# Strided PSUM writes for layer 0's aggregate and layer 1's turned sums in a two-layer graph attention kernel

## The chip, the cores and the metric

The kernel runs on one core of a Trainium2 chip. The metric is the device time of one execution in microseconds (us). The kernel before was timed three times: 2320.42, 2313.36 and 2315.58 us, median 2315.58. A core has five engines with a queue each: TensorE (PE; its weight loads are listed apart as PEld), VectorE (DVE), ScalarE (ACT), GpSimd (POOL) and SyncE (SP). Products of TensorE land in PSUM; VectorE and ScalarE move them from there to SBUF, which is called evicting them here.

## The reference

There are 16 graphs of 1024 nodes with 256 features, and an adjacency `adj` of zeros and ones per graph. Two layers follow each other, each with a residual and a layer norm around it:

```python
# layer 0, per graph
Wh  = h @ W.T
att = ei[:, None] + ej[None, :]          # ei = Wh @ a1, ej = Wh @ a2
att = bn(att); att = leaky(att); att = bn(att)
att = softmax(att, axis=2) * adj
h_prime = elu(bn(att @ Wh))              # batch norm over all graphs and nodes
x = layernorm(x + h_prime)

# layer 1, per graph and per head h of 4
fts    = x @ W[h]
coefs  = alpha * softmax(leaky(f1[:, None] + f2[None, :]) + mask(adj)) \
       + (1 - alpha) * softmax(adj)
out[h] = elu(coefs @ fts + x)
x = layernorm(x + mean_over_heads(out))
```

## The kernel before, in words

**Layer 0, the stage around the change (lines 523 to 656).** The scores are kept transposed, with keys on the 128 partitions. For graph b and key block k of 8, `weights(b, k)` makes a tile of 128 keys by 1024 queries: ScalarE scales (L534), VectorE takes the leaky maximum (L537), ScalarE exponentiates (L538), VectorE multiplies by the mask into `em` (L542, 11 buffers), and VectorE adds the unmasked weights into the running sum `sm` (L546, L548). `aggregate(b, hf, k)` multiplies: for each half `hf` of 512 queries and each half `oc` of the features, eight products over k accumulate into one PSUM bank `pa` (L578; four banks). A product in fp32 is recorded as two matmul instructions. `divisors(b)` sums `sm` over the partitions with 16 instructions (L555), takes the reciprocal on VectorE (L560), spreads it over all partitions by transposes of a broadcast column (L565), and ScalarE copies these from PSUM into `rd` (L570), two copies of 512 columns per graph. `store(b, hf)` evicts: VectorE multiplies each bank by `rd` with a sum as a by-product (L594), four times per graph, and ScalarE squares for the batch norm's variance (L603). The order of nodes in `hb` is permuted: query 8q + k is stored in column block k at place q. In the kernel before, L594 reads PSUM and `rd` in order and writes `hb` with a step of 128 elements.

The loop over b issues graph b's 16 groups of products with graph b+1's `weights` in between, `store(b - 1, 1)` after the second group, and `divisors(b + 1)` at the end. In this layer a planner, which works with estimated costs, arranges the instructions into each engine's queue before the launch; in layer 1 the order is written out by hand.

**Layer 1 (lines 1043 to 1849).** Only the neighbours are fetched: for each graph, lists of neighbours are built from the adjacency's bits (`Lists`), and rows of a table in DRAM are gathered by GpSimd's indirect DMA (L1341). A graph has 8 chunks `it`, each with 5 blocks of 25 nodes, and 4 heads in two pairs, so 16 units of (chunk, head pair), 256 units in all. Per unit: products of the weights with the fetched rows give sums `pu` (L1565); ScalarE divides them into `s` (L1631); `turn` multiplies each of the 5 blocks of `s` by the small matrix `MX`, which transposes the block and mixes the two softmaxes, into the one PSUM buffer `pt` (L1637, ten instructions of 100 columns); `turned` copies `pt` into `sT` on ScalarE (L1647); `linear` multiplies by the weights (L1659, eight instructions); VectorE adds x (L1667); ScalarE exponentiates (L1673); VectorE folds the heads (L1680 to L1688); the layer norm and the store follow. The loop at L1827 runs these as a pipeline: in step n, `turn` and `turned` work on unit n − 3, `linear` on unit n − 5, `add` and `exps` on unit n − 6.

In the kernel before, `pt` is laid out block by block (block, head, place), written in order by each product; `sT` needs node LO + 5q + n of a head at place (head, q, n), so the copy reads PSUM in order and writes SBUF with a step of five elements. Between the units stand the side works of the next graphs: scaling of eight node groups on ScalarE (L1485), the cast of list words (L1184), the residual's transposes (L1438) with their evictions (L1448, L1455), and the building of lists on VectorE. The last, rest block of each graph has its own turn (L1583), which the change leaves alone.

Of the kernel before, what the change touches and what calls it, by code (L numbers as in the profile page):

```python
# [8 lines left out]
F32 = mybir.dt.float32  # L9
# [10 lines left out]
P = 128  # L20
# [7 lines left out]
def kernel(  # L28
# [29 lines left out]
    nc = tc.nc  # L58
    B, N, F = x.shape
    H = W.shape[0]  # L60
    K = N // P
    C = F // P
    HALF = 512
    NH = N // HALF
# [46 lines left out]
    QB, NB = 25, 5  # L111
    NQ = K * NB + 1
    LEVELS = [1] * (NQ - 1) + [3]
    LO = 2
# [91 lines left out]
    with ExitStack() as l0:  # L206
# [10 lines left out]
        def small(pool, name, shape):  # L217
            return pool.tile([P, *shape], F32, name=name)
# [5 lines left out]
        with tc.tile_pool(name="apool", bufs=1) as apool, tc.tile_pool(  # L224
            name="aps", bufs=2, space=PSUM
# [14 lines left out]
            for name, v in (  # L240
# [3 lines left out]
                n = v.shape[0] // P  # L244
# [15 lines left out]
            for fc in range(C):  # L260
# [7 lines left out]
                for oc in range(C):  # L268
# [4 lines left out]
                        start=(oc == 0),  # L273
                        stop=(oc == C - 1),
# [4 lines left out]
            for b in range(B):  # L279
                wx = apool.tile([P, K, FX], F32, tag="wx", name=f"wx_{b}", bufs=3)  # L280
                for kk in range(K // KK):
# [10 lines left out]
                    for k in range(KK):  # L292
                        pw = aps_w.tile([P, FX], F32, tag="w", name=f"pw0_{b}_{kk}_{k}")
                        for fc in range(C):
                            nc.tensor.matmul(  # L295
                                pw, xT[:, k, fc, :], WX[:, fc, :],
                                start=(fc == 0), stop=(fc == C - 1),
# [26 lines left out]
        with tc.tile_pool(name="bpool", bufs=1) as bpool, tc.tile_pool(  # L324
            name="bps", bufs=2, space=PSUM
# [46 lines left out]
            q = small(qpool, "q", [K, B])  # L372
# [58 lines left out]
            for b in range(B):  # L431
# [17 lines left out]
                for k in range(K):  # L449
                    for it in range(K):  # L450
                        nc.tensor.matmul(
                            pt[:, k, 0:7], ds[it][:, k * P : (k + 1) * P], powers[:, b, it, 0:7],
                            start=(it == 0), stop=(it == K - 1),
# [69 lines left out]
        with tc.tile_pool(name="wk", bufs=1) as wk, tc.tile_pool(  # L523
            name="ps_a", bufs=4, space=PSUM
# [4 lines left out]
            ems, es, sm, rd, hb = ({} for _ in range(5))  # L529
# [21 lines left out]
            def divisors(b):  # L551

                pd = ps_s.tile([P, K], F32, tag="s", name=f"pd_{b}")
                for it in range(K):
                    nc.tensor.matmul(  # L555
                        pd[:, it : it + 1], sm[b][:, it * P : (it + 1) * P], ones[:, 0:1],
                        start=True, stop=True,
                    )
                r = wk.tile([P, K], F32, tag="rc", name=f"rc_{b}", bufs=2)
                nc.vector.reciprocal(r, pd)  # L560
                rd[b] = wk.tile([P, N], F32, tag="rd", name=f"rd_{b}", bufs=2)
                for hf in range(NH):
                    ps = ps_s.tile([P, HALF], F32, tag="s", name=f"prd_{b}_{hf}")
                    for k in range(KH):
                        nc.tensor.transpose(  # L565
                            ps[:, k * P : (k + 1) * P],
                            r[:, hf * KH + k : hf * KH + k + 1].to_broadcast([P, P]),
                            ident,
                        )
                    nc.scalar.copy(rd[b][:, hf * HALF : (hf + 1) * HALF], ps)  # L570

            acc = {}

            def aggregate(b, hf, k):
                for oc in range(C):
                    if k == 0:
                        acc[b, hf, oc] = ps_a.tile([P, HALF], F32, tag="a", name=f"pa_{b}_{hf}_{oc}")
                    nc.tensor.matmul(  # L578
                        acc[b, hf, oc],
                        wh[b][:, k, oc * P : (oc + 1) * P],  # L580
                        ems[b, k][:, hf * HALF : (hf + 1) * HALF],
                        start=(k == 0),
                        stop=(k == K - 1),
                    )

            def store(b, hf):
                if hf == 0:
                    hb[b] = wk.tile([P, C, N], F32, tag="hb", name=f"hb_{b}", bufs=2)
                half = slice(hf * HALF, (hf + 1) * HALF)
                part = hb[b].rearrange("p c (k q) -> p c k q", k=K)[:, :, :, hf * P // 2 : (hf + 1) * P // 2]  # L590
                n = b * NH + hf
                sums3 = wk.tile([P, C], F32, tag="sums3", name=f"sums3_{b}_{hf}", bufs=2)
                for oc in range(C):
                    nc.vector.tensor_tensor_reduce(  # L594
                        out=part[:, oc].rearrange("p k q -> p q k"),
                        in0=acc[b, hf, oc].rearrange("p (q k) -> p q k", k=K),
                        in1=rd[b][:, half].rearrange("p (q k) -> p q k", k=K), scale=1.0,
                        scalar=0.0, op0=ALU.mult, op1=ALU.add, accum_out=sums3[:, oc : oc + 1],
                    )
                nc.vector.tensor_scalar(mn3[:, n, :], sums3, -1.0 / HALF, None, ALU.mult)  # L600
                for oc in range(C):
                    dist = wk.tile([P, K, P // 2], BF16, tag="dist", name=f"dist_{b}_{hf}_{oc}", bufs=2)
                    nc.scalar.activation(  # L603
                        dist, part[:, oc], AF.Square, bias=mn3[:, n, oc : oc + 1], scale=1.0,
                        accum_out=sq3[:, n, oc : oc + 1],
                    )
                if hf == NH - 1:
                    nc.sync.dma_start(h_dram[b], hb[b])
# [7 lines left out]
            for b in range(B):  # L616
                for n in range(NH * K):
                    hf, k = divmod(n, K)
                    aggregate(b, hf, k)
                    if b == 0 and n == K + 2:  # L620
                        divisors(0)
                    if n == K + 4:
                        casts.behind(hb[b][0:1, 0, 0:1])
                    if n == 1 and b + 2 < B:
                        mts[b + 2] = mask(mpool, b + 2, "mt0")
                    if n == 1 and b > 0:
                        store(b - 1, NH - 1)
                    if n == (K + 1 if b else K + 3):
                        store(b, 0)
                    if n % 2 == 0 and b + 1 < B:  # L630
                        weights(b + 1, n // 2)
                    if n == 2 and b + 2 < B:
                        queries(b + 2)
                    if n == 3 and b == 4:
                        shifted1()
                if b + 1 < B:
                    divisors(b + 1)
                if b + 2 < B:
                    load(b + 2)
            store(B - 1, NH - 1)  # L640

            mv3 = wk.tile([P, C, 2], F32, name="mv3")
# [400 lines left out]
    with ExitStack() as l1:  # L1043
# [4 lines left out]
        ps_t = l1.enter_context(tc.tile_pool(name="ps_t", bufs=1, space=PSUM))  # L1048
# [12 lines left out]
        QR = (H + 1) * QB  # L1061
        MX = pk.tile([P, H, QB], F32, name="MX")
# [321 lines left out]
        class Graph:  # L1384
# [49 lines left out]
            def turn(self, k):  # L1434

                pz = self.pz[k] = ps_s.tile([P, C, TW], F32, tag="s", name=f"pz_{self.b}_{k}")
                for oc in range(C):
                    nc.tensor.matmul(  # L1438
                        pz[:, oc, :], self.h[:, oc, k * P : (k + 1) * P], IW[:, oc, :],
                        start=True, stop=True,  # L1440
                    )
# [153 lines left out]
        class Unit:  # L1595
# [36 lines left out]

            def turn(self):

                self.pt = ps_t.tile([P, NB, H, QB], F32, tag="t", name=f"pt_{self.nm}")
                for i in range(NB):
                    nc.tensor.matmul(  # L1637
                        self.pt[:, i].rearrange("p h q -> p (h q)"),
                        self.first.s[0:QR, i, self.hp * P : (self.hp + 1) * P],
                        MX[0:QR].rearrange("p h q -> p (h q)"), start=True, stop=True,  # L1640
                    )

            def turned(self):
                f, u = self.first, self.it
                if self.hp == 0:
                    f.sT = pk.tile([P, C, H, P], F32, tag="sT", name=f"sT_{self.nm}", bufs=2)
                nc.scalar.copy(  # L1647
                    f.sT[:, self.hp, :, LO : LO + NB * QB].rearrange("p h (q n) -> p n h q", n=NB), self.pt
                )
                if self.hp == 1:  # L1650
                    sl = self.g.sl[:, :, :, 3 * u : 3 * u + 3]
                    nc.scalar.copy(f.sT[:, :, :, 0:LO], sl[:, :, :, 0:LO])
                    nc.scalar.copy(f.sT[:, :, :, P - 1 : P], sl[:, :, :, LO:3])
# [96 lines left out]
        def side(g):  # L1750
# [11 lines left out]
            for hf in range(2):  # L1762
                after[AT["rw", hf]] += [each(lists.load_rows, hf)]
                turned(AT["words", hf], lists.words, lists.worded, hf)
            early[AT["used"]] += [lists.used]
            turned(AT["places"], lists.places, lists.placed)
            for part in range(4):
                early[AT["low"][part]] += [each(lists.low, part)]
# [128 lines left out]
```

## Time and profile before

| | |
|---|---|
| median of three runs | 2315.58 us |
| profiled execution, its own time | 2355.05 us |
| its span | 2353.3 us |
| mean granted TensorE clock | 0.924 |
| busy: TensorE, VectorE, ScalarE, GpSimd | 2032.3, 1851.5, 1537.4, 929.0 us |
| layer 0's products L578 | 323.8 to 832.8 us of the span |
| layer 1's turns L1637 | 949.4 to 2323 us of the span |
| L578, 512 columns | 1024 instructions |
| L594, 512 elements | 64 instructions, median 1049 ns |
| L570, 512 elements | 32 instructions, median 586 ns |
| L1637, 100 columns | 2560 instructions |
| L1647, 500 elements | 256 instructions, median 1059 ns |

[...]products overlap; how long one holds TensorE is read from the distance of the starts. The profiled execution is one single execution and was longer than the three timed ones.

### The profile page before, as it was taken

To read this page: it belongs to the slowest core of one execution; us is meant where nothing else is said; L and a number is where in the kernel's file an instruction comes from. 1 tells how busy PE (TensorE), PEld (TensorE's weight loads), DVE (VectorE), ACT (ScalarE), POOL (GpSimd) and SP (SyncE) were. 2 spreads that over 40 slices of the span, in tenths; PEclk is the share of its full clock that TensorE was granted. 3 is DMA by queue.
4 is the path that set the end of the run, shared out by engine and by line. 5 is a ranking of instruction groups with operands and counts; after the bars stand their busy time and mean duration, and the time that the engine had idled before them with its cause. 6 is when DMAs were issued, how large, how long until landed. Compare 5 with 4: busy or idle time off the path is not lost. (4 is left out here: it accounts for less than half of the span.)

```text
span 2353.3 us, 35722 instructions
## 1 busy us (share of the span) xinstructions
PE 2032.3 (86%) x12023; PEld 1572.7 (67%) x12023; DVE 1851.5 (79%) x4480; ACT 1537.4 (65%) x3156; POOL 929.0 (39%) x1005
## 2 busy tenths in 40 slices
PE   6685468999999943899999998999998999999995
PEld 5574334444444432787887887887887887887885
DVE  3234799999999754598889888798898888898885
ACT  1111667777777522668877877868877868868775
POOL 0000100000000004456667666666666657667671
PEclk9897569999999965899999999999999999999998
DMA  8697979996555134646756755756755756756550
GB/s 244 186 275 182 279 150 208 214 215 166 150 161 152 72 121 147 178 150 161 208 162 167 205 158 151 205 162 160 208 161 152 200 166 161 202 166 159 142 147 24
DMA packets 344669, 404.68 MB, mean 172 GB/s; under 512 B 189929, under 2 KB 291357, under 8 KB 334237
## 3 DMA queue, kind: packets, MB, share of 16 engines
q1 hardware_dynamic: 293533, 258.40, 38.1%
q0 software_dynamic: 49728, 141.39, 24.9%
q10 hardware_dynamic: 1216, 2.51, 0.3%
q8 instruction: 98, 1.61, 0.3%
q14 instruction: 94, 0.77, 0.1%
HBM read 330.90 MB, written 104.88 MB: 185 GB/s over the span
## 5 line engine op out<-in xcount | busy, mean ns | idle before, releaser
L1341 POOL DMA_INDIRECT xc<-xe_dram,ix x640 | 683.6, 1068 | 209.7 <-issue 173.7
L1659 PE MATMUL pv<-W1s,sT 128*128 128x256 f32 x2048 | 504.1, 390 | 1.8 <-issue 0.9
L578 PE MATMUL pa<-em,wh 128*128 128x512 f32 x1024 | 451.9, 599 | 18.1 <-issue 13.4
L1659 PEld LDWEIGHTS pv<-W1s,sT 128*128 128x128 f32 x2048 | 380.5, 196 | 45.6 <-issue 1.3
L1637 PEld LDWEIGHTS pt<-MX,s 125*128 125x128 f32 x2560 | 343.7, 202 | 44.7 <-ACT sT L1647 15.4
L578 PEld LDWEIGHTS pa<-em,wh 128*128 128x128 f32 x1024 | 194.2, 192 | 251.0 <-issue 240.1
L1637 PE MATMUL pt<-MX,s 125*128 125x100 f32 x2560 | 346.9, 285 | 15.3 <-ACT sT L1647 8.5
L1565 PE MATMUL pu<-xc,w 128*125 128x256 f32 x1280 | 348.7, 391 | 5.5 <-issue 4.5
L1647 ACT COPY sT<-pt 128x500 f32<-128x500 f32 x256 | 271.8, 1062 | 104.2 <-PE pt L1637 90.2
L1631 ACT ACTIVATE s<-pu,z 125x256 f32<-125x256 f32 x640 | 259.6, 472 | 44.3 <-DVE z L1623 27.8
L1673 ACT ACTIVATE m<-v,neg 128x512 f32<-128x512 f32 x256 | 183.7, 718 | 155.4 <-DVE v L1667 99.5
L1565 PEld LDWEIGHTS pu<-xc,w 128*125 128x125 f32 x1280 | 232.4, 191 | 42.7 <-issue 11.3
L534 ACT ACTIVATE e<-eb,c,s 128x1024 f32<-128x1024 f32 x128 | 155.0, 1236 | 80.2 <-DVE sm L548 41.9
L1716 POOL TENSOR_TENSOR ors<-ors,mhalf 128x1 f32<-128x1 f32 x128 | 105.7, 826 | 223.1 <-DVE ors L1710 216.4
L1667 DVE TENSOR_TENSOR v<-pv,x 128x512 f32<-128x512 f32 x256 | 175.0, 684 | 11.8 <-PE pv L1659 9.7
L538 ACT ACTIVATE e<-e,v,u 128x1024 f32<-128x1024 f32 x128 | 152.3, 1229 | 30.6 <-DVE e L537 24.5
L1438 PE MATMUL pz<-IW,h 128*128 128x136 f32 x512 | 89.7, 306 | 79.9 <-DVE fs L1455 37.7
L542 DVE TENSOR_TENSOR em<-e,mt 128x1024 f32<-128x1024 f32 x128 | 155.6, 1220 | 2.3 <-ACT e L538 1.3
L295 PE MATMUL pw<-WX,xT 128*128 128x266 f32 x512 | 130.5, 410 | 28.9 <-DVE wx L299 13.8
L537 DVE SCALAR_TENSOR_TENSOR e<-e 128x1024 f32<-128x1024 f32 x128 | 151.6, 1219 | 0.0
L299 DVE COPY wx<-pw 128x266 f32<-128x266 f32 x128 | 54.7, 434 | 117.3 <-PE pw L295 90.9
L291 ACT COPY xT<-px 128x512 f32<-128x512 f32 x64 | 34.5, 588 | 166.9 <-PE px L285 166.9
(301 smaller groups left out, 3180.5 us busy)
## 6 DMA issues: line engine op xcount, KB each, us to landing
x<-in_x_dram SPq DMA_DIRECT2D x32, 1024.0 KB
adj<-in_adj_dram POOLq DMA_DIRECT2D x16, 2048.0 KB
rw<-adj SPq DMA_DIRECT2D x32, 1024.0 KB
A<-u_dram SPq DMA_DIRECT2D x128, 250.0 KB
xe_dram<-x SPq DMA_DIRECT2D x16, 1060.0 KB
wh_dram<-wx SPq DMA_DIRECT2D x16, 1024.0 KB
wh<-wh_dram SPq DMA_DIRECT2D x16, 1024.0 KB
h_dram<-hb SPq DMA_DIRECT2D x16, 1024.0 KB
```

Source lines behind the costliest of these rows:

```text
L534: nc.scalar.activation(e, ebs[b], AF.Identity, bias=c1[:, k, b : b + 1], scale=s1[:, k : k + 1])
L538: nc.scalar.activation(e, e, AF.Exp, bias=v2[:, k : k + 1], scale=u2[:, k : k + 1])
L542: nc.vector.tensor_tensor(em, e, mts[b][:, k, :], ALU.mult)
L578: nc.tensor.matmul(acc[b, hf, oc], wh[b][:, k, oc * P : (oc + 1) * P], ems[b, k][:, hf * HALF : (hf + 1) * HALF], start=(k == 0), stop=(k ...
L1341: nc.gpsimd.indirect_dma_start(out=self.xc[:, i, :], out_offset=None, in_=xe_dram[g.b % 2], in_offset=bass.IndirectOffsetOnAxis(ap=g.l.ix[ ...
L1565: nc.tensor.matmul(pu[0:QR, 0:F], c.w[:, k].rearrange("p h q -> p (h q)"), c.xc[:, k, 0:F], start=(i == 0), stop=(i == len(OF[q]) - 1),)
L1631: nc.scalar.mul(f.s[0:QR, i], f.pu[i][0:QR, 0:F], f.z[0:QR, i : i + 1])
L1637: nc.tensor.matmul(self.pt[:, i].rearrange("p h q -> p (h q)"), self.first.s[0:QR, i, self.hp * P : (self.hp + 1) * P], MX[0:QR].rearrange ...
L1647: nc.scalar.copy(f.sT[:, self.hp, :, LO : LO + NB * QB].rearrange("p h (q n) -> p n h q", n=NB), self.pt)
L1659: nc.tensor.matmul(self.pv[:, hh, :], self.first.sT[:, fc, self.hp * HP + hh, :], W1s[:, fc, self.hp * HP + hh, :], start=(fc == 0), stop= ...
L1667: nc.vector.tensor_tensor(self.v2, self.pv, self.g.x[:, self.it].unsqueeze(1).to_broadcast([P, HP, F]), ALU.add)
L1673: nc.scalar.activation(self.m, self.v2, AF.Exp, bias=neg1, scale=1.0)
```

## The change

Both places get the same exchange of orders. The product writes its columns into PSUM with a step, at the place where the eviction will want them, and the eviction then reads and writes runs of neighbouring elements.

Layer 0: the bank `pa` is laid out as (k, q), 8 by 64. A product still reads its 512 query columns in order (q, then k), and writes them with a step of 64 elements. L594 then reads PSUM in order and writes runs of 64. Its second operand `rd` must have the same order, so L570 now reads PSUM with a step of eight elements and writes in order.

Layer 1: `pt` is laid out as (head, q, block). Each of the five block products writes its 100 columns with a step of five elements; L1647 reads PSUM in order and writes four runs of 125. The number of instructions, of bytes and of buffers stays as it was everywhere.

```diff
-                rd[b] = wk.tile([P, N], F32, tag="rd", name=f"rd_{b}", bufs=2)
+                rd[b] = wk.tile([P, NH, K, P // 2], F32, tag="rd", name=f"rd_{b}", bufs=2)
...
-                    nc.scalar.copy(rd[b][:, hf * HALF : (hf + 1) * HALF], ps)
+                    nc.scalar.copy(rd[b][:, hf], ps.rearrange("p (q k) -> p k q", k=K))
...
-                        acc[b, hf, oc] = ps_a.tile([P, HALF], F32, tag="a", name=f"pa_{b}_{hf}_{oc}")
+                        acc[b, hf, oc] = ps_a.tile([P, K, P // 2], F32, tag="a", name=f"pa_{b}_{hf}_{oc}")
                     nc.tensor.matmul(
-                        acc[b, hf, oc],
+                        acc[b, hf, oc].rearrange("p k q -> p q k"),
                         wh[b][:, k, oc * P : (oc + 1) * P],
-                        ems[b, k][:, hf * HALF : (hf + 1) * HALF],
+                        ems[b, k][:, hf * HALF : (hf + 1) * HALF].rearrange("p (q k) -> p q k", k=K),
...
                     nc.vector.tensor_tensor_reduce(
-                        out=part[:, oc].rearrange("p k q -> p q k"),
-                        in0=acc[b, hf, oc].rearrange("p (q k) -> p q k", k=K),
-                        in1=rd[b][:, half].rearrange("p (q k) -> p q k", k=K), scale=1.0,
+                        out=part[:, oc], in0=acc[b, hf, oc], in1=rd[b][:, hf], scale=1.0,
...
-                self.pt = ps_t.tile([P, NB, H, QB], F32, tag="t", name=f"pt_{self.nm}")
+                self.pt = ps_t.tile([P, H, QB, NB], F32, tag="t", name=f"pt_{self.nm}")
                 for i in range(NB):
                     nc.tensor.matmul(
-                        self.pt[:, i].rearrange("p h q -> p (h q)"),
+                        self.pt[:, :, :, i],
                         self.first.s[0:QR, i, self.hp * P : (self.hp + 1) * P],
-                        MX[0:QR].rearrange("p h q -> p (h q)"), start=True, stop=True,
+                        MX[0:QR], start=True, stop=True,
...
                 nc.scalar.copy(
-                    f.sT[:, self.hp, :, LO : LO + NB * QB].rearrange("p h (q n) -> p n h q", n=NB), self.pt
+                    f.sT[:, self.hp, :, LO : LO + NB * QB],
+                    self.pt.rearrange("p h q n -> p h (q n)"),
                 )
```

More of the change, by code (lines that the diff above doesn't have):

```diff
@@ L588, in store @@
                     hb[b] = wk.tile([P, C, N], F32, tag="hb", name=f"hb_{b}", bufs=2)
-                half = slice(hf * HALF, (hf + 1) * HALF)
                 part = hb[b].rearrange("p c (k q) -> p c k q", k=K)[:, :, :, hf * P // 2 : (hf + 1) * P // 2]
```

## The prediction

> **What bounds the kernel now.** I read the page's groups first (columns: line, engine, operation, tiles and shape, count | busy us, mean ns | idle us before them and what ended it), for the operations that the diff touches and for two undisturbed yardsticks.
>
> ```profile
> L578 PE MATMUL pa<-em,wh 128*128 128x512 f32 x1024 | 451.9, 599 | 18.1 <-issue 13.4
> L1637 PE MATMUL pt<-MX,s 125*128 125x100 f32 x2560 | 346.9, 285 | 15.3 <-ACT sT L1647 8.5
> L1647 ACT COPY sT<-pt 128x500 f32<-128x500 f32 x256 | 271.8, 1062 | 104.2 <-PE pt L1637 90.2
> L1438 PE MATMUL pz<-IW,h 128*128 128x136 f32 x512 | 89.7, 306 | 79.9 <-DVE fs L1455 37.7
> L291 ACT COPY xT<-px 128x512 f32<-128x512 f32 x64 | 34.5, 588 | 166.9 <-PE px L285 166.9
> ```
>
> L1647 copies 500 elements in 1062 ns where L291 copies 512 in 588: the strided SBUF write costs some 0.48 us. Next, TensorE's timeline in layer 0 (start us, length us, what, and in brackets the idle time before it):
>
> ```profile
> 406.90 26.77 PE L578 MATMUL pa<-em,wh 128*128 128x512 f32 x62
> 434.29 1.92 PE L555 MATMUL pd<-ones,sm 128*128 128x1 f32 x16 [0.62 <-DVE sm L548]
> 436.07 1.10 PE L578 MATMUL pa<-em,wh 128*128 128x512 f32 x2
> 437.01 1.04 PE L565 MATMUL prd<-ident,rc 128*128 128x128 f32 x8
> 437.88 26.77 PE L578 MATMUL pa<-em,wh 128*128 128x512 f32 x62
> 465.29 1.92 PE L555 MATMUL pd<-ones,sm 128*128 128x1 f32 x16 [0.63 <-DVE sm L548]
> ```
>
> A graph takes 30.99 us, and TensorE is without work for 0.6 us of it, waiting for VectorE's last sum. So two engines stand almost level: VectorE sets the pace, and TensorE's own 30.4 us is the floor just below. A product takes 26.77/62 = 0.43 us, or 0.84 ns a column.
>
> Then the same timeline in layer 1, for what interrupts TensorE within one graph of 88 us, and VectorE's timeline for the stall that comes before:
>
> ```profile
> 1521.25 1.36 PE L1637 MATMUL pt<-MX,s 125*128 125x100 f32 x10 [0.60 <-ACT sT L1647]
> 1536.56 0.32 PE L1200 MATMUL pp<-act,tri 128*128 128x369 bf16 x1 [1.67 <-DVE act L1192]
> 1544.93 0.73 PE L1438 MATMUL pz<-IW,h 128*128 128x136 f32 x4 [1.65 <-DVE sl L1578]
> 1552.44 0.70 PE L1438 MATMUL pz<-IW,h 128*128 128x136 f32 x4 [2.21 <-DVE fs L1455]
> ```
>
> ```profile
> 1504.96 0.19 DVE L1188 TENSOR_REDUCE wl<-pc 128x8 f32<-128x32 f32 x1 [4.76 <-ACT wd L1184]
> ```
>
> TensorE works about 94% of layer 1; most of its gaps are waits for a late VectorE, which itself had stood 4.76 us behind ScalarE's queue (eight L1485 scalings, then the cast L1184) and ran without a real pause from there. From 950 to 2323 us the stages' busy times are 1286 us TensorE, 1159 VectorE and 1047 ScalarE of 1373.
>
> [...] No matmul of the kernel before writes PSUM with a stride[...]. [...] L578 records two instructions per product (1024 for 512), each at twice the bf16 time per column (below). [...] L594 in the trace steps by 0.91 us for 512, so 1.78.
>
> **The disputed price: a strided PSUM write.** Two lines bear on it, both TensorE's:
>
> ```profile
> 1481.54 4.96 PE L1266 MATMUL po<-hA,B 128*128 128x64 f16 x48
> 1536.72 0.32 PE L1201 MATMUL pp<-act,far 128*128 128x369 bf16 x1
> ```
>
> L1201 starts 0.16 us after the 369 columns of L1200: 0.43 ns a column of bf16, written in order. [...] An fp32 product delivers one column per 0.84 ns. [...] by this estimate the stride costs nothing in fp32. Against it: L1266 reads its moving operand from SBUF with a stride and takes 1.7 ns a column (48 products, 2752 columns, 4.8 us). Were a strided PSUM write as slow, L578 would go from 0.43 to 0.87 us. I take zero, with +0.44 us as the other end; a gain is excluded, since the contiguous write already streams at the fp32 rate.
>
> **Part by part.**
> Layer 0, VectorE: L594, 64 times. Its input reads stay sequential and its output now is runs of 64. L1448, the same operation on 256 elements from PSUM, reaches its accumulator read 0.35 us after its start; another 256 at 1.04 ns make 0.62. So 0.91 becomes 0.62: −0.29 us, four per graph, −1.2 us.
> Layer 0, ScalarE: L570, 32 times, now reads PSUM with a step of eight elements. No row shows it: between 586 ns (unchanged) and 1062 (as L1647). I take 0.8 us, +0.2. ScalarE is busy 319 of 444 us here and the consumer L594 runs ten products later, so it is hidden. Queued behind it are the next graph's exponentials L538, for which VectorE's L542 waits; VectorE then has 1.2 us per graph to spare, which covers 2 × 0.48. It is uncovered only in the first graph, up to +0.9 us. The change adds no instruction, transfer or wait anywhere.
> Layer 0, TensorE: the 1024 products at zero. VectorE's pace falls to 29.8 us, below TensorE's 30.4; so of the 1.2 us only the 0.62 wait is won, in 12 of the 16 graphs: −7.4. At both ends (TensorE's 4.6 us wait for the first L594, the last pair before the batch norm) −0.6 each, the first given back to L570. Layer 0: −8. Layer 1's first rows are loaded after layer 0's end, so this moves through.
> Layer 1, TensorE: ten 100-column products per unit follow each other at 0.11 us[...]; 100 columns at 0.84 ns are 0.084 us. Zero here too, and even a stride that cost 25% would hide.
> Layer 1, ScalarE: L1647 now reads PSUM in order and writes four runs of 125: 588 ns less 12 elements, 0.58 us. −0.48 us × 256 = −123 us of ScalarE, nearly all off the path, since 90 us of its idle time are already waits for these very products. On the path: (a) TensorE idles 15.3 us ahead of L1637, in pieces of 0.15 to 0.65 us; PSUM has one such buffer, and 0.48 us less takes about two thirds, −10. (b) One copy stands in the chain before the cast that VectorE waits for (−0.5 per graph), and VectorE's waits for L1425's scaling, 20.5 us in all, go (−1.3 per graph): VectorE gets 1.8 us ahead, of which TensorE, itself 0.65 earlier, gains 1.1 in its 3 us of waits for VectorE per graph; 15 × 1.1 = −16, and I take −13, since other bursts are not shortened. (c) The drain has one copy on its chain, −1. What is late next is VectorE's own burst of list building. Layer 1: −24.
> Sum: −32 us against the profiled execution's 2355.05. That one lies 39.5 us above the median of 2315.58, so the share scales by 0.983: −31, **2284 us**.
>
> **Rivals.**
> (1) The stride is slow (the other side). Place: L578's write. Price: 1024 × 0.44 = +450 us in layer 0, and in layer 1 2560 × (0.17 − 0.11) = +154. With nothing gained, about 2900 us. [...] It decides from 32/1024 = 31 ns per product on, 7%. A part-price of 30 to 120 ns gives 2315 to 2420.
> (2) The gain is hidden: TensorE is already at its floor, ScalarE's time was idle anyway, the bursts keep their length, L570 delays the exponentials. Then only the 7 us of layer 0 at most are left, eaten by layer 0's planner placing instructions differently for changed access patterns: 2309 to 2322. Against it: the waits named are real gaps of TensorE.
> (3) The change doesn't speed the passes: L1647's slowness might lie in its three-level pattern. Against: L1549, only 125 elements with the same stride, takes 375 ns where 200 in order (L1591) take 319. Time 2307 to 2315, and it goes with (2).
>
> **How the numbers follow.** What this measurement tells from no change is about 0.3%, 7 us. Likeliest case 0.74, by itself 2260 (layer 1 giving 45 and layer 0 12) to 2304 (8 and 4); rivals 2 and 3 together 0.05; slow stride 0.21, a third of it part-price. The range from 2258 to 2335 holds nearly all of the first two and the beginning of the part-price, about 0.8; what is left out is the slow stride itself. Faster 0.74, same 0.05, slower 0.21.
>
> **What would show it.** Right: L578's 62 products still take 26.8 us; L594 steps by 0.62 us; the wait ahead of L555 is gone and the graph takes 30.4 us; L1647 at 0.58 us and the idle time ahead of L1637 under 6 us; L1637 still at 0.11 us. Wrong: L578 over 0.46 us a product, or ten L1637 products over 1.2 us. If those hold but the waits for VectorE ahead of L1438 stay at 3 us per graph, the error lies in (b).

## The result, and the profile after

The kernel after takes 2296.59 us (median of nine runs) against 2319.96 us for the kernel before (nine runs). The ratio is 0.9906, with a 95% interval of 0.9888 to 0.9924: 0.94% faster, or 21.8 us of 2320; the slowest of the nine (2307.92) lies below the fastest of the kernel before (2313.36). Forecast were 31 us and "faster".

The profiled execution of the kernel after took 2298.42 us. That of the kernel before, on which the prediction worked, took 2355.05 and was not a typical one, as the first experiment shows; the difference of the two profiled executions, 57 us, is therefore not the effect of the change.

In the code after, the lines from L594 on have moved: L594 is L593, L1200 is L1197, L1438 is L1435, L1455 is L1452, L1578 is L1575, L1637 is L1634, L1647 is L1644. The page's groups, those that answer to the groups shown before (same columns):

```profile
L578 PE MATMUL pa<-em,wh 128*128 128x512 f32 x1024 | 452.0, 599 | 17.7 <-DVE em L542 13.4
L1634 PE MATMUL pt<-MX,s 125*128 125x100 f32 x2560 | 351.4, 286 | 5.4 <-ACT sT L1644 3.0
L1644 ACT COPY sT<-pt 128x500 f32<-128x500 f32 x256 | 144.2, 563 | 110.9 <-PE pt L1634 110.9
L1435 PE MATMUL pz<-IW,h 128*128 128x136 f32 x512 | 90.2, 308 | 56.7 <-DVE fs L1452 33.1
```

The disputed price is settled by the first line: 1024 strided instructions have 452.0 us of busy time, where the same ones in order had 451.9. In both kernels they are recorded at 599 ns each and start 0.43 us apart (62 in 26.77 us), so that they overlap. The turns' mean is 286 ns against 285. That says less: they follow each other at 0.11 us in both kernels, as the sums L555 with a single column do (16 in 1.8 us), while their 100 columns at 0.84 ns make 0.084 us; by this estimate up to about 0.03 us more per instruction would not have shown in layer 1. The copy has lost its 0.5 us (563 ns against 1062), ScalarE waits for the turns all the longer (110.9 us), and TensorE's idle time ahead of the turns went from 15.3 to 5.4 us.

The evictions of layer 0, in the views of their lines (shortest, median and longest duration in ns):

```profile
L593 DVE CUSTOM_DVE_ANT_0 hb<-pa,rd x64: 636/684/691, 363.8 to 820.3; 128x512 f32<-128x512 f32 x64
L593 DVE DVE_READ_ACCUMULATOR2_ANT sums<- x64: 77/82/84, 364.4 to 820.9; 128x1 f32 x64
L570 ACT COPY rd<-prd x32: 564/587/592, 360.5 to 798.0; 128x512 f32<-128x512 f32 x32
```

L593's median is 684 ns, where L594's was 1049. From start to start within a pair it takes 0.61 and 0.56 us in turn, where it took 0.90 and 0.85. Its accumulator read also got shorter, from 152 ns in the kernel before to 82:

```profile
L594 DVE DVE_READ_ACCUMULATOR2_ANT sums<- x64: 135/152/165, 366.6 to 834.4; 128x1 f32 x64
```

L570, which now reads PSUM with a step of eight elements, takes 587 ns where it took 586: the step costs it nothing.

TensorE's timeline in layer 0:

```profile
404.70 26.77 PE L578 MATMUL pa<-em,wh 128*128 128x512 f32 x62
431.31 1.84 PE L555 MATMUL pd<-ones,sm 128*128 128x1 f32 x16
433.02 1.10 PE L578 MATMUL pa<-em,wh 128*128 128x512 f32 x2
433.96 1.04 PE L565 MATMUL prd<-ident,rc 128*128 128x128 f32 x8
434.83 26.77 PE L578 MATMUL pa<-em,wh 128*128 128x512 f32 x62
461.44 1.84 PE L555 MATMUL pd<-ones,sm 128*128 128x1 f32 x16
```

The brackets, the waits for VectorE's last sum, are gone. A graph takes 461.44 − 431.31 = 30.13 us, where it took 30.99, and nothing interrupts TensorE: it is the floor of this stage now. And its waits in layer 1, in one graph as in the prediction:

```profile
1486.76 0.47 PE L1197 MATMUL pp<-act,tri 128*128 128x369 bf16 x1 [2.10 <-DVE act L1189]
1495.12 0.73 PE L1435 MATMUL pz<-IW,h 128*128 128x136 f32 x4 [0.57 <-DVE sl L1575]
1502.63 0.70 PE L1435 MATMUL pz<-IW,h 128*128 128x136 f32 x4 [2.21 <-DVE fs L1452]
```

The wait for L1452 has the same 2.21 us as before. Together with the waits for L1575 it comes to 48.5 us in layer 1, 3.2 us for each of 15 graphs. The prediction had named this, waits that stay at 3 us per graph, as the sign of an error in its step (b).

### The profile page after: what moved, and what is told of

The parts are those of the page before. It is cut to its first block, busy times and chain, and to the rows that moved or that the text cites. A ratio compares the mean times of both kernels' runs of the same rounds, so it can differ in the third digit from the quotient of the medians.

```text
span 2296.6 us, 35722 instructions
## 1 busy us (share of the span) xinstructions
PE 2026.6 (88%) x12023; PEld 1578.7 (69%) x12023; DVE 1833.9 (80%) x4480; ACT 1441.7 (63%) x3156; POOL 938.0 (41%) x1005
## 5 line engine op out<-in xcount | busy, mean ns | idle before, releaser
L578 PE MATMUL pa<-em,wh 128*128 128x512 f32 x1024 | 452.0, 599 | 17.7 <-DVE em L542 13.4
L1634 PEld LDWEIGHTS pt<-MX,s 125*128 125x128 f32 x2560 | 350.6, 204 | 30.7 <-ACT sT L1644 9.8
L578 PEld LDWEIGHTS pa<-em,wh 128*128 128x128 f32 x1024 | 193.7, 192 | 251.0 <-issue 235.6
L1634 PE MATMUL pt<-MX,s 125*128 125x100 f32 x2560 | 351.4, 286 | 5.4 <-ACT sT L1644 3.0
L1628 ACT ACTIVATE s<-pu,z 125x256 f32<-125x256 f32 x640 | 261.5, 474 | 82.8 <-DVE z L1620 57.4
L1644 ACT COPY sT<-pt 128x500 f32<-128x500 f32 x256 | 144.2, 563 | 110.9 <-PE pt L1634 110.9
L1714 POOL TENSOR_TENSOR ors<-ors,mhalf 128x1 f32<-128x1 f32 x128 | 110.8, 865 | 202.1 <-DVE ors L1708 200.7
L1665 DVE TENSOR_TENSOR v<-pv,x 128x512 f32<-128x512 f32 x256 | 174.9, 683 | 10.9 <-PE pv L1657 10.5
L542 DVE TENSOR_TENSOR em<-e,mt 128x1024 f32<-128x1024 f32 x128 | 155.7, 1218 | 3.4 <-PE pa L578 2.1
L1435 PE MATMUL pz<-IW,h 128*128 128x136 f32 x512 | 90.2, 308 | 56.7 <-DVE fs L1452 33.1
```

The source lines that it names most:

```text
L542: nc.vector.tensor_tensor(em, e, mts[b][:, k, :], ALU.mult)
L578: nc.tensor.matmul(acc[b, hf, oc].rearrange("p k q -> p q k"), wh[b][:, k, oc * P : (oc + 1) * P], ems[b, k][:, hf * HALF : (hf + 1) * HAL ...
L1628: nc.scalar.mul(f.s[0:QR, i], f.pu[i][0:QR, 0:F], f.z[0:QR, i : i + 1])
L1634: nc.tensor.matmul(self.pt[:, :, :, i], self.first.s[0:QR, i, self.hp * P : (self.hp + 1) * P], MX[0:QR], start=True, stop=True,)
L1665: nc.vector.tensor_tensor(self.v2, self.pv, self.g.x[:, self.it].unsqueeze(1).to_broadcast([P, HP, F]), ALU.add)
```

## The experiments

The comparisons were made in four sets. The kernel before took 2320 us in the set of the result, 2315 in that of the next four experiments, and 2345 and 2346 in the last two; so only ratios to the kernel before of the same set are compared.

**The kernel before once more.** No edit.

> The kernel before, unchanged, profiled a second time: its first profiled execution took 2355.05 us and lies 35 us above the median of nine timed runs (2319.96). If that surplus was an accident of the one execution, this one takes 2313 to 2325 us, and the stretch between layer 0's last product and the first turn of layer 1 (832.8 to 949.4 us then, 116.6 us) shrinks towards the 100 us of the kernel after (819.6 to 919.6). If the profile itself costs time in this kernel, it is again about 2355.

It took 2311.99 us, and layer 1's first turn came 99.2 us after layer 0's last product ended (836.1 to 935.3). So the surplus was an accident of the one execution. In the first profile that stretch was 17 us longer, with TensorE once waiting 9.1 us for something that the profile doesn't name, and layer 1 from its first turn to its last was 29 us longer (1373.5 us against 1344.9), so that the prediction's figures for layer 1 come from an unusually long one. Where before and after are compared by their waits below, this second profile is used.

**Each layer's part alone.** `l0_only` has the diff's hunks up to `store`, `l1_only` those of `turn` and `turned`.

> Only layer 0's part: strided products L578, L570 reading PSUM with a step, L594 in runs; layer 1 as before. Theory (TensorE was 0.6 to 0.9 us per graph behind VectorE's pace, and a strided fp32 write costs nothing): 12 us less than before, ratio 0.995; a graph takes 30.13 us. Rival (the two parts split as the prediction's sum had it): 8 us less, 0.9965. If the stride had a price in layer 0 that layer 1 pays back: 0 or slower.

> Only layer 1's part: strided products L1637, copy L1647 in runs; layer 0 as before. Theory (TensorE gets back its waits for the one PSUM buffer of the turns, about 10 us, and its waits for a late VectorE stay): 10 us less than before, ratio 0.9957. Rival (VectorE also gets ahead, as the prediction's step b had it): 24 us less, 0.99. Copy L1647 0.56 us in both.

Layer 0 alone: 0.9934 (0.9915 to 0.9953), 15 us of 2315. Layer 1 alone: 0.9960 (0.9942 to 0.9978), 9 us. The two add up to some 24.5 us, against 21.8 for the whole, within the intervals, so nothing speaks for the parts helping or hindering each other. Layer 0 gave more than the prediction had (8) and layer 1 less (24); both figures lie outside the intervals. TensorE's waits in layer 1, from the views of its waits (who waited for whom, us in total, times, longest), first of the kernel before in its second profile:

```profile
PE pz L1438 <- DVE fs L1455: 34.7, 15, 3.7
PE pz L1438 <- DVE sl L1578: 19.2, 15, 1.6
PE pt L1637 <- ACT sT L1647: 18.7, 31, 1.5
```

and of layer 1's part alone:

```profile
PE pz L1438 <- DVE fs L1455: 31.2, 15, 3.8
PE pz L1438 <- DVE sl L1578: 19.2, 14, 1.6
...
PE pt L1637 <- ACT sT L1647: 4.0, 3, 2.1
```

The wait for the one PSUM buffer of the turns loses 14.7 us; the two waits for VectorE ahead of L1438 together lose 3.5 of 53.9. The profile of layer 1's part is of one of its fastest executions (2297.49, median 2304.47), so the waits have lost more here than the median time has.

**What a strided write costs a faster stream.** The products of `places` are in bf16 and write 369 columns:

```diff
-                self.pp = pp = ps_s.tile([P, K + 1, NQ], F32, tag="s", name=f"pp_{self.b}")
+                ppt = ps_s.tile([P, NQ, K + 1], F32, tag="s", name=f"pp_{self.b}")
+                self.pp = pp = ppt.rearrange("p q k -> p k q")
```

> The kernel before, but the bf16 products L1200, L1201 and L1203 write their PSUM bank with a step of nine elements (places innermost by block instead of by column), and what reads it reads with that step; same results. Theory [...]: the 369 columns of L1200, 0.16 us from its start to that of L1201 before, now take 0.31 us. Rival 1 (a strided write is free at any rate): 0.16 us. Rival 2 (a stride costs as much as the strided read of L1266, 1.7 ns a column): 0.63 us. The time of the whole moves by less than 5 us in all cases.

TensorE's timeline of this kernel (L1201 and L1202 are the L1200 and L1201 of the kernel before):

```profile
1244.29 0.47 PE L1201 MATMUL pp<-act,tri 128*128 128x369 bf16 x1
1244.56 0.51 PE L1202 MATMUL pp<-act,far 128*128 128x369 bf16 x1
1244.87 1.46 PE L1204 MATMUL pp<-act,ones 128*128 128x41 bf16 x8
```

The second product holds TensorE for 1244.87 − 1244.56 = 0.31 us, as the theory had it (369 columns at the 0.84 ns of the fp32 products). In order it held it for 1536.88 − 1536.72 = 0.16, by the line of the kernel before that follows those in the prediction:

```profile
1536.88 0.82 PE L1203 MATMUL pp<-act,ones 128*128 128x41 bf16 x8
```

The first holds TensorE for 0.27 us, somewhat less than the theory's 0.31, where it was 0.16, and its recorded median grows by 0.153 us, from 318 to 471 ns. These distances are the same in 14 of the 16 graphs; in the first two all are longer, in both kernels. So a stride is not free as such: with it the second product took 0.84 ns a column and the first 0.73, where both took 0.43 in order; and 0.84 ns is what the fp32 products took in order as well. What sets this rate is not shown: no other step was tried in bf16. The whole took 2321.0 us in one execution, 6 us above the median of its set where less than 5 was expected; one execution can't tell that from chance, since fourteen of the kernel before ranged over 11 us.

**Does VectorE's backlog matter?** Two theories of TensorE's waits for L1452 and L1575 stand against each other. Theory A, as in the prediction: VectorE is late because it stood still earlier, behind ScalarE's cast. Theory B: VectorE is late because its queue has other work ahead of these evictions in the same step. Four edits of the kernel after test them. The first moves the cast behind which VectorE stood:

```diff
-                nc.scalar.copy(
+                nc.vector.tensor_copy(
                     self.wd[:, :, hf * n : (hf + 1) * n].rearrange("p k (q n) -> p k q n", q=KH),
```

> The kernel after, with the cast of the list words (L1181) on VectorE instead of ScalarE, so that VectorE no longer waits 4.4 us per graph behind ScalarE's queue for it; VectorE works 0.3 us twice per graph more. Theory A (VectorE's backlog from that stall is what TensorE later waits for ahead of L1435): these waits, 48 us in all after, fall under 15 us, 25 to 35 us less than after, 0.978 of before. Theory B (the waits are set by VectorE's order within the step, where list work stands ahead of the evictions that free the two PSUM buffers): they stay at 40 us or more, time as after within 6 us, 0.990 of before.

0.9852 (0.9824 to 0.9880). VectorE no longer stands behind ScalarE for the cast (60.4 us in all after, none here), but the stall is only shortened: VectorE now stands 33.4 us ahead of the cast itself and 17.0 us ahead of L1521 (2.9 in the kernel after). TensorE's waits ahead of L1435 go from 29.8 to 27.7 us for L1452 and from 18.7 to 12.4 for L1575. That the greater one hardly moves speaks for theory B. The time could not tell: the interval holds neither theory's figure, and the kernel after was not among these runs.

The second moves the two evictions themselves to ScalarE:

```diff
-                nc.vector.tensor_copy(self.fs[:, k], self.pz[k][:, :, P:TW])
+                nc.scalar.copy(self.fs[:, k], self.pz[k][:, :, P:TW])
...
-                nc.vector.tensor_scalar(self.s[0:QR], self.pu[0:QR, 0:F], z[0:QR], None, ALU.mult)
+                nc.scalar.mul(self.s[0:QR], self.pu[0:QR, 0:F], z[0:QR])
```

> The kernel after, with the scaling L1575 and the copies L1452 on ScalarE instead of VectorE; ScalarE has about 120 us more idle time than in the kernel before and stands idle when TensorE waits. Theory A: VectorE loses 1.9 us of work per graph, TensorE gains about that, 25 us, 0.980 of before. Theory B: the wait for L1575 (19 us in all) goes down to some 5, the wait for the residual's eviction stays since L1445 is on VectorE still; 10 to 15 us less than after, 0.985 of before.

0.9861 (0.9835 to 0.9887). The waits only changed their name: 32.4 us for ScalarE's L1452 and 16.9 for its L1575, where theory B expected some 5 for the latter. In 12 of the 15 graphs the wait for L1452 is a little shorter, 1.73 us for 2.21, but two of 6.2 and 5.0 us at the start of layer 1 take that back. L1445, which must read the same PSUM buffer, is still VectorE's. The ratio lies near theory B's 0.985 and off theory A's 0.980, but as the kernel after itself had 0.9870 in the next set, it shows no gain.

The third spreads the products over the steps, the fourth adds the second to it:

```diff
             'mean': (-17, -14), 'elu': (-26, -25, -24, -23), 'turn': (-22, -21, -19,
-            -19, -18, -17, -15, -15), 'gather': -4, 'turn last': 0,
+            -18, -17, -16, -15, -15), 'gather': -4, 'turn last': 0,
```

> The kernel after, with the residual's eight transposes L1435 in steps -22, -21, -19, -18, -17, -16, -15, -15 of the graph's schedule instead of -22, -21, -19, -19, -18, -17, -15, -15: one pair of products in one step fewer, so that two PSUM buffers suffice there. Theory A: no change, as VectorE is as late as before. Theory B: the 2.2 us wait per graph ahead of L1435 goes, 26 us less than after, 0.979 of before, and if only half of it goes, 0.985.

> The two last edits together on the kernel after. Theory B: the gains add, 35 to 40 us less than after, 0.974 of before. Theory A: as the edit of L1575 and L1452 alone.

0.9874 (0.9849 to 0.9899) and 0.9892 (0.9865 to 0.9918). The waits for L1452 and L1575 disappear in the third, as theory B had it, but another takes their place (the single 9.7 us lie at the start of layer 1):

```profile
PE pt L1634 <- ACT sT L1644: 33.8, 18, 2.7
PE pz L1435 <- ACT sTl L1588: 9.7, 1, 9.7
PE pt L1634 <- ACT s L1628: 7.8, 15, 0.6
```

TensorE now waits for ScalarE's copy again (50.4 us in the fourth). No gain came of either, and the expected 0.979 and 0.974 were missed. Why the copy becomes late when the transposes are spread was not tried.

**VectorE's order within the step.** The last set has the kernel after itself, the first edit again, and an edit that moves only VectorE's order: the list work L1224 behind the evictions of the same step.

> The kernel after, unchanged, beside the next three on one chip, since the kernel before took 2345 us on the chip of the last comparisons and 2315 on the first. The ratio to the kernel before should be 0.989 to 0.992 here too; TensorE's waits ahead of L1435 about 48 us.

> The cast L1181 on VectorE once more, beside the kernel after. Its waits ahead of L1435 were 40 us of the 48 although VectorE's stall was gone, so theory B expects no more than 8 us less than after (the waits for the list products L1197 and a few short ones), ratio to before 0.987 to 0.991; theory A, that the stall matters, 0.978 to 0.984.

```diff
-            for part in range(4):
-                early[AT["low"][part]] += [each(lists.low, part)]
...
                 early[AT["turn"][k] + 1] += [each(g.beside, k)]
+            for part in range(4):
+                early[AT["low"][part]] += [each(lists.low, part)]
```

> The kernel after, with the four list steps `low` (L1224) placed behind the residual's evictions L1445 and L1452 of the same step in VectorE's order instead of ahead of them; nothing else moves. Theory B (TensorE's 2.2 us wait per graph ahead of L1435 is VectorE doing 1.8 us of L1224 first): this wait falls from 30 us in all to under 8; time 0 to 20 us less than after, 0 if a wait for ScalarE's copy L1644 takes its place as it did where the transposes were spread. Theory A (backlog): the wait stays.

> Both edits. If VectorE's order and its stall are two separate limits, the gains add: 0.978 to 0.986 of before. If layer 1 is held by VectorE's and ScalarE's loop as a whole, no more than the cast alone: 0.987 to 0.991.

The kernel after has 0.9870 (0.9835 to 0.9906) here, a little below the 0.989 expected but with that inside the interval. The cast on VectorE has 0.9886 (0.9850 to 0.9922): no difference, which is what theory B expected. The new order has 0.9817 (0.9784 to 0.9851), and with the cast 0.9826 (0.9794 to 0.9858). That lies in the range expected if two gains add, but the order alone reaches it, so the cast adds nothing that these runs can tell. In six runs each, the slowest of the new order (2306.33 us) lies below the fastest of the kernel after (2306.55); the medians are 2299.01 and 2309.60. VectorE's timeline in the kernel after shows what stood ahead, and in its first line a pause earlier in the graph:

```profile
1481.10 0.42 DVE L1445 CUSTOM_DVE_ANT_0 x<-pz,x 128x256 f32<-128x256 f32 x1 [3.26 <-DMA x<-in_x_dram]
...
1500.24 1.82 DVE L1224 TENSOR_TENSOR B<-low,lanes 128x1536 f16<-128x1536 f16 x2
1501.97 0.42 DVE L1445 CUSTOM_DVE_ANT_0 x<-pz,x 128x256 f32<-128x256 f32 x1
1502.32 0.08 DVE L1445 DVE_READ_ACCUMULATOR2_ANT mv<- 128x1 f32 x1
1502.32 0.17 DVE L1452 COPY fs<-pz 128x16 f32<-128x16 f32 x1
```

L1452 ends at 1502.49 and L1435 starts at 1502.63: TensorE's 2.21 us are mostly the 1.82 us of L1224 ahead of the eviction. How long VectorE had stood still earlier made no difference between these two graphs: in this one it was 4.42 us for the cast, up to 1455.81, and another 3.26 for a load, up to 1481.10; in the next it was 4.39 for the cast and none for a load, and TensorE's wait was 2.21 us in both. With the new order, TensorE's waits in one graph:

```profile
1505.87 0.73 PE L1435 MATMUL pz<-IW,h 128*128 128x136 f32 x4 [1.65 <-DVE sl L1575]
1511.65 0.70 PE L1435 MATMUL pz<-IW,h 128*128 128x136 f32 x4 [0.47 <-DVE fs L1452]
1514.30 0.83 PE L1634 MATMUL pt<-MX,s 125*128 125x100 f32 x4 [0.87 <-ACT s L1628]
```

The wait for L1452 falls to 0.47 us here, and in all from 29.3 us in the kernel after of this set to 5.7. A new one of up to 0.9 us for the divided sums L1628 (10.0 in all) takes a part back, and some 10.6 us remain as a gain. This is the version that beats both kernels.

## Why the prediction was right, and where it was not

**The mechanism and the sign.** The price of the strided write was taken as zero from two numbers of the trace, the bf16 stream in order (0.43 ns a column) and the fp32 rate (0.84). The step from these two to a free stride was the author's estimate: no trace had shown a strided write by then. The price is zero for L578 (452.0 us of busy time with the step, 451.9 in order). At the turns none shows either (286 ns against 285, and 0.11 us apart in both), but a small one would be hidden there, as the prediction itself said. The bf16 experiment measured the rate that the estimate needs, and not only the result: 0.84 ns a column in the second product and 0.73 in the first, with a step of nine elements. What sets that rate was not shown.

**Layer 0.** The term was undersized: −8 predicted, about −15 measured (10.9 to 19.7 by the interval). VectorE's step fell as estimated: by 0.29 us, from 0.90 and 0.85 to 0.61 and 0.56. (The estimate's 1.04 ns an element is close to what other lines of the kernel before show: L542 takes 1220 ns for 1024 elements and L1667 684 for 512, 1.05 ns for each element more.) The error lies in TensorE's floor. I took 30.4 us from the recorded wait of 0.62, but that wait is counted from the recorded end of the last product, and where nothing waits the next group starts 0.16 us before that end (404.70 + 26.77 is 431.47, and the next group starts at 431.31). The sums L555 were also some 0.07 us shorter without a wait ahead of them: the product after them starts 1.71 us later, where it was 1.78. The floor is 30.13 us, so 0.86 us per graph came free, about 12 us over 14 graphs; the interval holds these 12 us and leaves the other 3 open. That the planner might disturb the order (rival 2) did not show: in the two profiles TensorE, ScalarE and GpSimd run their instructions in the same order throughout, and VectorE does in layer 0.

**Layer 0's ScalarE** at 0.8 us per copy was wrong, and harmless: the strided read of PSUM cost nothing (587 ns against 586).

**Layer 1, step (a)** predicted −10 for the waits for the turns' buffer. They lost 14.7 us in the one profile of layer 1's part alone, whose time fell by 9 (5 to 13). So the step is right, and its size agrees with the time. **Step (c)**, 1 us, is too small for these runs to show.

**Layer 1, step (b)** failed. It said that VectorE would get ahead by 1.8 us per graph and that TensorE would gain 1.1 of it in its waits for VectorE. VectorE's waits did shrink as it said: for L1425's scaling from 20.5 to 3.9 us and for the cast from 66.4 to 58.7, from the second profile of the kernel before to that of layer 1's part alone. But TensorE's waits for L1455 and L1578 lost only 3.5 us in all. The greater one is not a backlog carried over from the stall some 45 us earlier, as I read the uninterrupted timeline. It arises in the step itself: two PSUM buffers, and 1.82 us of list work standing ahead of the eviction in VectorE's queue. Shortening the stall left it, changing the order took it away. Its length could have told: in the first profile of the kernel before it is 2.21 or 2.22 us in 13 of 15 graphs. Why TensorE waits for L1578, up to 1.65 us per graph, was not settled.

**The sum** was 31 us against 21.8. Layer 0 gave 7 us more than predicted and layer 1 15 less, and these partly cancelled: the sign was reasoned, but that the sum came so close is in part luck. Rival 1 is refuted for L578. Rival 2's point, that ScalarE's saved time was mostly idle anyway, holds for layer 1: of 128 us of copies saved, 9 us of time came out. Rival 3 is refuted: both passes became faster.

## What to carry to other kernels

Before exchanging the order of a PSUM write and its eviction, compare the product's time per column in order with the 0.84 ns that a strided column took here. The fp32 products, at 0.84 ns a column anyway, were written with a step of 64 elements for nothing, while L594 stepped 0.29 us faster and L1647 took 0.5 us less; the bf16 products of 369 columns, at 0.43 ns in order, went from 0.16 us to 0.27 and 0.31. What the saved time was worth was decided by the wait that ended last: 128 us of copies saved in layer 1 were worth 9 us. Where a wait has the same length in nearly every round, as the one for L1455 had, look first at what stands directly ahead of the instruction that frees the buffer, before suspecting a backlog.

## What the runs showed of the hardware

- A PSUM write with a step of nine elements holds TensorE for 0.31 us in the second of two bf16 products of 369 columns and 0.27 in the first, where both hold it for 0.16 in order. An fp32 instruction of 512 columns takes 0.43 us with a step of 64 elements as in order, 0.84 ns a column.
- Fp32 products that follow each other stood 0.11 us apart with 100 columns (L1637) as with one (L555).
- ScalarE reads PSUM with a step of eight fp32 elements as fast as in order (587 and 586 ns for 512). Writing SBUF with a step of five, in rows of 25, its copy of 500 elements takes 1062 ns, and 563 in runs of 125.
- VectorE's L594, 512 elements from PSUM, takes 0.90 and 0.85 us from start to start when it writes with a step of 128 elements, and 0.61 and 0.56 in runs of 64. The accumulator read behind it took 152 ns with the step and 82 with runs.
